# A graph layer on one core: the ReLU moves to VectorE, destinations' rows come from a table, 44 copied columns a step, updates part by part, a ring of twenty

## Chip, core and metric

One core of a Trainium2 chip. The metric is the device time of one execution in microseconds (us), lower is better; the kernel before was timed in three runs.

## What is computed

A graph layer over N = 12500 nodes of 64 features and E = 212500 edges, which come sorted by destination. The reference, cut to what matters:

```python
msg_in = concatenate([nodes[row], nodes[col], edge_features], axis=-1)   # 64 + 64 + 32
messages = relu(msg_in @ mW1 + mb1) @ mW2 + mb2                           # 128 hidden, 64 out
aggregated = segment_sum(messages, col, num_segments=12500)
upd = relu(concatenate([nodes, aggregated]) @ uW1 + ub1) @ uW2 + ub2
out = layernorm(x + upd)                                                  # no scale, eps 1e-5
```

Here `row` is the source of an edge (`src`), `col` its destination (`dst`). All data are fp32.

## The kernel before

**Groups.** Edges are worked in their order in G = 554 groups of 384 (three tiles of 128; the last group has two tiles, one of 20). Since edges are sorted, the destinations of a group lie in a window of W = 32 consecutive nodes. The kernel's host part passes the first destination of each group; a check on the chip (`ordered_edges`) finds out whether the windows hold, and another routine, `unordered`, runs if not. With these inputs `ordered` does the work.

**A step.** TensorE's work is written out by hand in steps. Step k does `turn(k)`, `hidden(k-2)` and `sums(k-4)`, each with its PSUM banks in two copies (`own.ps[g % 2]`). A step's first matmul carries all waits, and those who follow wait for its last one.

- `gather(g)` (L146 to 157): POOL fetches the source rows of a group with one indirect DMA per tile of 128 edges into `own.s`, a ring of RING = 8 groups; it is written AHEAD = 4 steps ahead. A new turn of the ring waits until the `turn` that read the old rows is done.
- `onehot(g)` (L329, VectorE): the place of each edge in its window as a one-hot row of 32, written beside the gathered rows.
- `turn(g)` (L341): TensorE transposes the 96 columns (64 features, 32 places) of each tile; ScalarE copies the result from PSUM into `own.st` (L351), where the edge features (`inputs`, L289) already lie below.
- `hidden(g)` (L366): one matmul per tile of `own.st` with `own.wm[g % 8]`. `wm` holds mW1's rows for the source (64), 32 rows with the projections of the window's nodes, and mW1's rows for the edge features (32). So the one-hot picks the destination's projection. ScalarE applies the ReLU into `own.h` (L377).
- `sums(g)` (L394, L399): matmuls of `h` with the one-hot add the group's hidden rows by destination, and count its edges. VectorE adds the window into `agg` (L406) and into a row of `own.xc` (L407), at a place taken from a register (`starts`, loaded by `places`).
- `places(b)` and `windows(b)`: for each block of four groups VectorE copies 4 x 32 nodes out of the transposed nodes `xc` (L308), TensorE projects them at the end of a step (L315), and VectorE copies 4 x 32 rows into `wm` (L320).

**Copied columns.** For some groups (`COPIED`) the first tile is not gathered. Its 128 columns are copied one by one from the transposed nodes `own.xc` to `own.st`, at addresses that are loaded into registers from a list of indices: `fetch(k)` (L475 to 507) has VectorE load 8 registers, copy 8 columns, load 12, copy 12, and ScalarE load 12, copy 12, load 8, copy 8 (VCOLS, ACOLS; loads L490, copies L503 and L505). COLS = 40 columns a step make a tile every 3.2 steps; 164 groups are served so. It begins with step 18 and ends before the last ten (SHORT), in which a step is cut into shorter ones.

**Updates.** When all edges of a chunk of 512 nodes are surely summed (`plan`), the update of the chunk is spread over steps (`step_update`): `load` brings the nodes, `first` does two matmuls (L424, L425), a ReLU on ScalarE (L427) and an add on VectorE (L428), `second` the outer matmuls (L437), an add (L439), the statistics (L443, L444) and a square root on ScalarE (L446), `third` scales (L451, L454) and stores (L458). Within one part an engine that follows waits for the one before it, in front of its own work for the step.

**Queues.** Each engine works its instructions in the written order. POOL has only the gathers after the start. SP issues the loads of edge features, of the nodes and source indices (`bit`, in the first 16 steps), of the lists, and the stores.

Of the kernel before, what the change touches and what calls it, by code (L numbers as in the profile page):

```python
# [34 lines left out]
AHEAD = 4  # L35
RING = AHEAD + 4
BLOCKS = 3
NW = 2 * SB
NH = 3
# [5 lines left out]
NEAR_GROUPS = 24  # L45
# [4 lines left out]
VCOLS = (8, 12)  # L50
ACOLS = (12, 8)
# [28 lines left out]
PLAN = plan()  # L80
COPIED = []
# [4 lines left out]
class Own:  # L86
# [4 lines left out]
    def __init__(self, nc, ctx):  # L91
# [10 lines left out]
        self.xc = on("own_xc", P, NP)  # L102

# [5 lines left out]
def ordered(ctx: ExitStack, tc: tile.TileContext, a, own, ok):  # L109
# [6 lines left out]
    xwp = ctx.enter_context(tc.tile_pool(name="xw", bufs=2))  # L116
# [6 lines left out]
    xc = own.xc[: D + 2]  # L123
    xc_bytes = own.xc.bitcast(U8)
# [20 lines left out]

    def gather(g):  # L146
        s = own.s[g % RING]
        loads[g] = [
            nc.gpsimd.indirect_dma_start(  # L149
                out=s[:p, j, :D], out_offset=None, in_=x[:, :],  # L150
                in_offset=bass.IndirectOffsetOnAxis(
                    ap=src_sb[:p, g * TG + j : g * TG + j + 1], axis=0),
            )
            for j, p in enumerate(tiles_of(g)) if j or g not in columned
        ]
        for i in loads[g]:
            after(i, *([turn_by[g // 2 * 2 + 1 - RING]] if g >= RING else []))
# [27 lines left out]
    nc.sync.dma_start(xc[D : D + 1, :].rearrange("o (p n) -> o p n", p=P), zero)  # L185
    nc.sync.dma_start(xc[D + 1 :, :].rearrange("o (p n) -> o p n", p=P), ones[:, : NP // P])
    w1b = const.tile([D + 2, H], F32, name="w1b")
    nc.vector.memset(w1b[D : D + 1, :], 0.0)
    nc.scalar.dma_start(w1b[:D, :], a["mW1"][D : 2 * D, :])
    nc.scalar.dma_start(w1b[D + 1 :, :], a["mb1"][None, :])  # L190
# [22 lines left out]
    nc.vector.memset(high[:, :NEAR_GROUPS], float(NEAR_NODES - W))  # L213
# [22 lines left out]
    ub1 = const.tile([H, 1], F32, name="ub1")  # L236
    nc.scalar.dma_start(ub1, a["ub1"][:, None])
    u2 = const.tile([H, D], F32, name="u2")
    nc.scalar.dma_start(u2, a["uW2"])
    u2b = const.tile([P, D], F32, name="u2b")  # L240
    nc.scalar.dma_start(u2b, a["ub2"][None, :].to_broadcast([P, D]))
    agg = const.tile([P, NP], F32, name="agg")
# [4 lines left out]
    starts, xws, indices, columns_by = {}, {}, {}, {}  # L247
# [3 lines left out]
    def combined():  # L251
# [5 lines left out]
        nc.vector.tensor_copy(ux[D : D + 1, :], wps[0:1, 1])  # L257
# [38 lines left out]
    def places(b):  # L296
# [8 lines left out]
        xw = xwp.tile([D + 2, SB, W], F32, name="xw")  # L305
        for i in range(n):
            starts[g + i] = v[i]
            nc.vector.tensor_copy(xw[:, i, :], xc[:, bass.ds(v[i], W)])  # L308
        xws[b] = xw, n

    def windows(b, wp, own_bank=True):


        xw, n = xws.pop(b)
        did = nc.tensor.matmul(wp[: n * W, :], xw[:, :n, :], w1b, start=True, stop=True)  # L315

        def copies():
            for i in range(n):
                g = b * SB + i
                c = nc.vector.tensor_copy(wm[g % NW][D : D + W, :], wp[i * W : (i + 1) * W, :])  # L320
                after(c, *([did] if own_bank else []), *([hidden_by[g - NW]] if g >= NW else []))
                wm_by[g] = c

        return did, copies
# [10 lines left out]
    def turn(g, ps):  # L335
# [9 lines left out]
        def copy(step):  # L345
# [5 lines left out]
                after(nc.scalar.activation(t[r, c : c + n][:, m], xt[r, m], AF.Copy), step)  # L351
# [9 lines left out]
    def hidden(g, ps):  # L361
# [11 lines left out]
        def relu(step):  # L373
            hidden_by[g] = step
            h = own.h[g % NH]
            if len(set(sizes)) == 1:
                relu_by[g] = [nc.scalar.activation(h, pre, AF.Relu)]  # L377
            else:
                relu_by[g] = [nc.scalar.activation(h[:p, j, :], pre[:p, j, :], AF.Relu)
                              for j, p in enumerate(sizes)]  # L380
# [6 lines left out]
    def sums(g, ps):  # L387
# [14 lines left out]
        def add(step):  # L402
            sums_by[g] = step
            at = bass.ds(starts.pop(g), W)
            return [
                after(nc.vector.tensor_tensor(agg[:, at], sg[:, 0, :], agg[:, at], ALU.add), step),  # L406
                after(nc.vector.tensor_tensor(xc[D : D + 1, at], counted,  # L407
                                              xc[D : D + 1, at], ALU.add), step),
            ]
# [3 lines left out]
    def update(base, p, n):  # L413
# [3 lines left out]
        def load():  # L417
            xin = up.tile([P, 4, D], F32, name="xin")
            nc.sync.dma_start(xin[:p, :n], x[rows, :].rearrange("(p n) d -> p n d", p=p))
            return xin  # L420

        def first(xin):
            u_ps = ups.tile([H, CH], F32, name="u_ps")
            nc.tensor.matmul(u_ps[:, :q], wc, agg[:, rows], start=True, stop=False)  # L424
            nc.tensor.matmul(u_ps[:, :q], ux, xc[: D + 1, rows], start=False, stop=True)  # L425
            u = up.tile([H, CH], F32, name="u")
            nc.scalar.activation(u[:, :q], u_ps[:, :q], AF.Relu, bias=ub1)  # L427
            nc.vector.tensor_tensor(xin[:p, :n], xin[:p, :n],  # L428
                                    u2b[:p].unsqueeze(1).to_broadcast([p, n, D]), ALU.add)
            return xin, u  # L430

        def second(xu):
            xin, u = xu
            o_ps = ups.tile([H, CH], F32, name="u_ps")[:, : 4 * D].rearrange(
                "p (n d) -> p n d", n=4)
            for k in range(n):
                nc.tensor.matmul(o_ps[:p, k], u[:, k:q:n], u2, start=True, stop=True)  # L437
            y = up.tile([P, 4, D], F32, name="y")
            nc.vector.tensor_tensor(y[:p, :n], o_ps[:p, :n], xin[:p, :n], ALU.add)  # L439
            stats = up.tile([P, 4, nc.vector.BN_STATS_DIM], F32, name="stats")  # L440
            mv = up.tile([P, 4, nc.vector.BN_AGGR_DIM], F32, name="mv")
            for k in range(n):
                nc.vector.bn_stats(stats[:p, k], y[:p, k])  # L443
                nc.vector.bn_aggr(mv[:p, k], stats[:p, k])  # L444
# [4 lines left out]
        def third(ymr):  # L449
# [10 lines left out]
        return [load, first, second, third]  # L460
# [14 lines left out]
    def fetch(k):  # L475
# [4 lines left out]
        if n == 0:  # L480
            indexes(i + 1)
        if n == SPAN - 2:
            addresses(i + 1)
        c0 = (k - BEGIN) * COLS
        for engine, count in [*((ET.DVE, c) for c in VCOLS), *((ET.Activation, c) for c in ACOLS)]:
# [9 lines left out]
            for q, at in zip(range(c0, c0 + count), v):  # L495
# [10 lines left out]
                after(by[engine], *([hidden_by[g - BLOCKS * SB]] if new else []))  # L506
            c0 += count
# [16 lines left out]
    def step(*work):  # L524
# [9 lines left out]
        copies = None  # L534
        for part, g, *_ in parts:
            if part is sums:
                for b in [b for b in xws if (b - 1) * SB <= g][:1]:
                    last, copies = windows(b, own.ps[g % 2][2][:, (TIMES + 1) * W :][:, :H])
                    did.append(last)
        for i in did[:-1]:  # L540
            tc.no_tile_sem_insts.add(i.ins.name)
            tc.add_to_no_dep_group("quiet", i.ins)
        for part, g, _, _, follow in parts:
            if part is sums:
                step_update(g)
            users[part][g % 2] = follow(did[-1])
            if part is sums and copies:
                copies()
                users[part][g % 2] += [wm_by[b * SB + i] for i in range(min(SB, G - b * SB))]
# [6 lines left out]
    windows(0, ups.tile([H, CH], F32, name="u_ps")[:, :H], False)[1]()  # L556
    indexes(0)
    made = summed = 0

    for k in range(G):  # L560
        if k < BITS:
            bit(k)
        if k == CHECKED:
# [361 lines left out]
```

## Time and profile before

| what | us |
|---|---|
| median of three runs | 1898.23 (1897.33 to 1900.16) |
| the profiled execution's own time | 1895.48 |
| its span (first to last instruction of the program) | 1893.5 |
| VectorE's wait for registers and the like ahead of L503 ("issue") | 217.9 |
| ScalarE's idle time ahead of the turn's copy (L351) | 205.8 |
| TensorE's idle time ahead of the transposes (L341) | 496.0 |
| granted TensorE clock, mean | 0.969 |

A group's row of the profile tells line, engine, operation, output from input, shape, the number of instructions, busy time and mean duration in ns, and then the engine's idle time just before them with what ended most of it ("issue": nothing that the profile shows). The timeline has start and length in us, with runs of like instructions merged; the brackets hold the idle time before. PE is TensorE's matmul row, PEld its weight loads, DVE VectorE, ACT ScalarE; a q behind the name is the engine's instruction queue.

### The profile page before, as it was taken

To read this page: it belongs to the slowest core of one execution; us is meant where nothing else is said; L and a number is where in the kernel's file an instruction comes from. 1 tells how busy PE (TensorE), PEld (TensorE's weight loads), DVE (VectorE), ACT (ScalarE), POOL (GpSimd) and SP (SyncE) were. 2 spreads that over 40 slices of the span, in tenths; PEclk is the share of its full clock that TensorE was granted. 3 is DMA by queue.
4 is the path that set the end of the run, shared out by engine and by line. 5 is a ranking of instruction groups with operands and counts; after the bars stand their busy time and mean duration, and the time that the engine had idled before them with its cause. 6 is when DMAs were issued, how large, how long until landed. Compare 5 with 4: busy or idle time off the path is not lost. (4 is left out here: it accounts for less than half of the span.)

```text
span 1893.5 us, 58044 instructions
## 1 busy us (share of the span) xinstructions
PE 1361.4 (72%) x12209; PEld 1193.4 (63%) x12209; DVE 1492.9 (79%) x13761; ACT 1550.7 (82%) x11818; POOL 1417.6 (75%) x1504
## 2 busy tenths in 40 slices
PE   3776777677777777677676776877767767767777
PEld 3666666666666666666665666666666656666665
DVE  3578888778888788887888878878888887888873
ACT  3489889888888888988988888889888888898882
POOL 7777777777777777777777777777777777777774
PEclk9999999999999999999999999999999999999999
DMA  6322222222222222222222222222222222222221
GB/s 136 73 46 45 46 48 44 50 43 48 46 45 48 47 43 50 45 46 44 48 50 43 48 46 45 46 48 44 50 44 47 47 48 44 47 44 50 44 47 29
DMA packets 68440, 92.50 MB, mean 49 GB/s; under 512 B 30893, under 2 KB 38350, under 8 KB 68078
## 3 DMA queue, kind: packets, MB, share of 16 engines
q0 software_dynamic: 47904, 49.12, 14.7%
q1 hardware_dynamic: 19260, 39.12, 7.4%
q14 instruction: 260, 2.13, 0.4%
q8 instruction: 102, 1.67, 0.4%
q10 hardware_dynamic: 914, 0.46, 0.1%
HBM read 85.29 MB, written 3.20 MB: 47 GB/s over the span
## 5 line engine op out<-in xcount | busy, mean ns | idle before, releaser
L149 POOL DMA_INDIRECT own_s<-in_x,src_sb x1497 | 1416.8, 946 | 457.3 <-issue 407.5
L503 DVE COPY own_st<-own_xc 64x4 uint8 x10500 | 897.7, 190 | 231.0 <-issue 217.9
L505 ACT ACTIVATE own_st<-own_xc 64x4 uint8 x10492 | 1057.1, 194 | 18.2 <-issue 15.2
L341 PE MATMUL own_ps<-own_ident,own_s 128*96 128x128 f32 x1661 | 289.5, 285 | 496.0 <-DMA own_s<-in_x,src_sb 157.9
L341 PEld LDWEIGHTS own_ps<-own_ident,own_s 128*96 128x96 f32 x1661 | 169.3, 132 | 566.1 <-ACT own_h L377 240.7
L394 PE MATMUL own_ps<-own_s,own_h 128*128 128x128 f32 x3322 | 480.5, 283 | 4.1 <-ACT own_h L377 2.9
L366 PE MATMUL own_ps<-own_wm,own_st 128*128 128x128 f32 x3322 | 479.4, 283 | 0.0
L351 ACT ACTIVATE own_st<-own_ps 96x384 f32<-96x384 f32 (+2 forms) x718 | 293.2, 408 | 205.8 <-PE own_ps L399 104.7
L394 PEld LDWEIGHTS own_ps<-own_s,own_h 128*128 128x128 f32 x3322 | 432.6, 199 | 6.3 <-ACT own_h L377 4.7
L366 PEld LDWEIGHTS own_ps<-own_wm,own_st 128*128 128x128 f32 x3322 | 432.1, 199 | 1.4 <-issue 0.5
L377 ACT ACTIVATE own_h<-own_ps 128x384 f32<-128x384 f32 x553 | 263.9, 477 | 16.0 <-PE own_ps L366 16.0
L399 PE MATMUL own_ps<-own_s,own_one 128*1 128x32 f32 x3322 | 190.1, 194 | 0.0
L320 DVE COPY own_wm<-own_ps 32x128 f32<-32x128 f32 x550 | 156.9, 285 | 5.6
L399 PEld LDWEIGHTS own_ps<-own_s,own_one 128*1 128x1 f32 x3322 | 114.5, 84 | 69.4 <-issue 6.2
L329 DVE TENSOR_TENSOR own_s<-iota,dlc 128x96 f32<-128x96 f32 x554 | 142.4, 258 | 14.3 <-issue 0.2
L406 DVE TENSOR_TENSOR agg<-own_ps,agg 128x32 f32 x554 | 105.1, 190 | 59.5 <-PE own_ps L399 25.9
L407 DVE TENSOR_TENSOR own_xc<-own_ps,own_xc 1x32 f32 x554 | 101.2, 183 | 30.6 <-PE u_ps L425 11.4
L308 DVE COPY xw<-own_xc 66x32 f32 x554 | 73.0, 207 | 15.5 <-DMA own_xc<-in_xT 9.8
L315 PE MATMUL own_ps<-w1b,xw 66*128 66x128 f32 (+1 forms) x276 | 69.1, 333 | 0.0
L446 ACT ACTIVATE rstd<-mv,eps 128x4 f32<-128x4 f32 (+1 forms) x25 | 7.4, 297 | 55.3 <-DVE mv L444 55.3
L437 PE MATMUL u_ps<-u,u 128*128 128x64 f32 (+1 forms) x196 | 50.1, 399 | 0.5 <-ACT u L427 0.5
L437 PEld LDWEIGHTS u_ps<-u,u 128*128 128x128 f32 (+1 forms) x196 | 47.1, 324 | 2.2 <-ACT u L427 0.9
(62 smaller groups left out, 276.7 us busy)
## 6 DMA issues: line engine op xcount, KB each, us to landing
own_st<-in_efT SPq DMA_DIRECT2D x138, 192.0 KB
own_s<-in_x,src_sb POOLq DMA_INDIRECT x1497
xin<-in_x SPq DMA_DIRECT2D x24, 128.0 KB
out<-o SPq DMA_DIRECT2D x24, 128.0 KB
own_xc<-in_xT SPq DMA_DIRECT2D x12, 179.2 KB
index<-in_src_copied SPq DMA_DIRECT2D x65, 1.2 KB
dlc_i<-in_dst_cols SPq DMA_DIRECT2D x1, 831.0 KB
own_xc<-in_xT SPq DMA_DIRECT2D x4, 179.5 KB
```

Source lines behind the costliest of these rows:

```text
L149: nc.gpsimd.indirect_dma_start(out=s[:p, j, :D], out_offset=None, in_=x[:, :], in_offset=bass.IndirectOffsetOnAxis(ap=src_sb[:p, g * TG + ...
L320: c = nc.vector.tensor_copy(wm[g % NW][D : D + W, :], wp[i * W : (i + 1) * W, :])
L329: places_by[g] = nc.vector.tensor_tensor(own.s[g % RING][:, :, D:], iota.unsqueeze(1).to_broadcast([P, TG, W]), dlc[:, g * TG : (g + 1) * ...
L341: nc.tensor.transpose(xt[:, j * P : j * P + p], s[:p, j, :], ident[:p, :p])
L351: after(nc.scalar.activation(t[r, c : c + n][:, m], xt[r, m], AF.Copy), step)
L366: nc.tensor.matmul(pre[:p, j, :], t[:, c + j * P : c + j * P + p], wm[g % NW], start=True, stop=True)
L377: relu_by[g] = [nc.scalar.activation(h, pre, AF.Relu)]
L394: did.append(nc.tensor.matmul(sg, h[:p, j, :], s[:p, j, D:].unsqueeze(1).to_broadcast([p, TIMES, W]), start=j == 0, stop=j == len(sizes) - 1))
L399: did.append(nc.tensor.matmul(counted, own.one[:p], s[:p, j, D:], start=j == 0, stop=j == len(sizes) - 1))
L406: after(nc.vector.tensor_tensor(agg[:, at], sg[:, 0, :], agg[:, at], ALU.add), step),
L503: by[engine] = nc.vector.tensor_copy(o, x_at)
L505: by[engine] = nc.scalar.activation(o, x_at, AF.Copy)
```

## The change

1. **ReLU.** VectorE applies it (`tensor_scalar` with max) instead of ScalarE.
2. **Columns.** VectorE 12 and 8, ScalarE 12 and 12: COLS = 44. VectorE's first twelve registers are loaded ahead of the add into `agg` (the list `between`), behind the ReLU; its first twelve copies come before the one-hot, the eight others after it. The list's load and address work go to the end of a step. `ordered_by_steps` takes the tool's own dependencies from the copies, which the steps order already.
3. **Destinations.** All nodes are projected once in 25 chunks of 512 (`projected`): one in each of the first 25 steps, two of them before, through the PSUM bank of the updates and ScalarE to a table in DRAM. For each group SP loads the 32 rows of its window into `wm` four steps ahead of its turn (`window`), at a row number from a register of SP. `LIMITS` keeps early windows within what is already in the table. The copies of nodes, the windows' matmul and the copies into `wm` go.
4. **Updates.** Six parts, one a step, each for one engine: `inner`, `relu`, `outer`, `stats`, `root`, `scaled`. The node and the bias enter the outer product by a matmul with an identity (`same`), so the load of the nodes and two adds go; the counts have a row of their own (COUNT) and a third inner matmul. The statistics are read from PSUM.
5. **Ring.** RING = 20, AHEAD = 16; a gather waits for the turn of its own slot.

`unordered` gets some of its space from `own.agg`; it isn't run here.

```diff
-AHEAD = 4
+AHEAD = 16
 RING = AHEAD + 4
-VCOLS = (8, 12)
-ACOLS = (12, 8)
+VCOLS = (12, 8)
+ACOLS = (12, 12)
...
-            after(i, *([turn_by[g // 2 * 2 + 1 - RING]] if g >= RING else []))
+            after(i, *([turn_by[g - RING]] if g >= RING else []))
...
+    def projected(c):
+        base, n = TABLE[c]
+        ps = ups.tile([H, CH], F32, name="u_ps").rearrange("p (n h) -> p n h", n=4)
+        for j in range(n):
+            nc.tensor.matmul(ps[:, j], xc[: D + 1, base + j : base + n * P : n], w1b,
+                             start=True, stop=True)
+        t = rowp.tile([P, 4, H], F32, name="t")
+        nc.scalar.activation(t[:, :n], ps[:, :n], AF.Copy)
+        written.append(after(nc.sync.dma_start(
+            by_dst[base : base + n * P, :].rearrange("(p n) h -> p n h", n=n), t[:, :n])))
+
+    def window(g):
...
+        wm_by[g] = nc.sync.dma_start(wm[g % NW][D : D + W, :],
+                                     by_dst[bass.ds(rows_at.pop(g), W), :])
+        after(wm_by[g], *written, *([hidden_by[g - NW]] if g >= NW else []))
+        written.clear()
...
-                relu_by[g] = [nc.scalar.activation(h, pre, AF.Relu)]
+                relu_by[g] = [nc.vector.tensor_scalar(h, pre, 0.0, None, ALU.max)]
...
+            count = xc[COUNT : COUNT + 1, at]
+            if between:
+                between.pop()()
+            a = after(nc.vector.tensor_tensor(agg[:, at], sg[:, 0, :], agg[:, at], ALU.add), step)
+            return [a, after(nc.vector.tensor_tensor(count, counted, count, ALU.add), step)]
...
         if k < G - SHORT:
+            between.append(lambda: registers(k, 0))
             step((turn, k), *([(hidden, k - 2)] if k > 1 else []),
                  *([(sums, k - 4)] if k > 3 else []))
             made, summed = max(0, k - 1), max(0, k - 3)
+            if between:
+                between.pop()()
+            fetch(0)
...
+        window(k + SB)
         onehot(k + 2)
-        fetch(k)
+        if k < G - SHORT:
+            for part in range(1, len(VCOLS + ACOLS)):
+                registers(k, part)
+                fetch(part)
```

More of the change, by code (lines that the diff above doesn't have):

```diff
@@ L144, in after, with ordered_by_steps @@
         return first
+    before = {}
+    def ordered_by_steps(i):
+        engine = i.ins.engine
+        tc.declare_no_dep(i.ins, group="features", keep=before.get(engine, []),
+                          reason="TensorE's step has read what the last turn of the ring wrote")
+        tc.add_to_no_dep_group("features", i.ins)
+        before[engine] = [i.ins]
+        return i
     def gather(g):
@@ L415, in update, with inner @@
         rows, q = slice(base, base + p * n), p * n
[L417 to L422, printed above, removed]
+        def inner():
             u_ps = ups.tile([H, CH], F32, name="u_ps")
             nc.tensor.matmul(u_ps[:, :q], wc, agg[:, rows], start=True, stop=False)
-            nc.tensor.matmul(u_ps[:, :q], ux, xc[: D + 1, rows], start=False, stop=True)
-            u = up.tile([H, CH], F32, name="u")
[L427 to L435, printed above, removed]
-            for k in range(n):
[L437 to L440, printed above, removed]
+            nc.tensor.matmul(u_ps[:, :q], ux, xc[: D + 1, rows], start=False, stop=False)
@@ L458, in third @@
             nc.sync.dma_start(out[rows, :].rearrange("(p n) d -> p n d", p=p), o[:p, :n])
-        return [load, first, second, third]
+        return [inner, relu, outer, stats, root, scaled]
     def indexes(i):
@@ L555, in ordered @@
     places(0)
-    windows(0, ups.tile([H, CH], F32, name="u_ps")[:, :H], False)[1]()
+    projected(0)
+    projected(1)
+    for g in range(SB):
+        window(g)
     indexes(0)
     made = summed = 0
+    between, held = [], {}
     for k in range(G):
```

154 lines of the change are left out of this document (83 added, 71 removed).

## The prediction

> **What bounds the kernel now.** I read the page's table of groups first, because its idle column tells who waits, then the instructions of the gather line alone, then the timeline of a few steps and of the end.
>
> ```profile
> PE 1361.4 (72%) x12209; PEld 1193.4 (63%) x12209; DVE 1492.9 (79%) x13761; ACT 1550.7 (82%) x11818; POOL 1417.6 (75%) x1504
> L149 POOL DMA_INDIRECT own_s<-in_x,src_sb x1497 | 1416.8, 946 | 457.3 <-issue 407.5
> L503 DVE COPY own_st<-own_xc 64x4 uint8 x10500 | 897.7, 190 | 231.0 <-issue 217.9
> ```
> By busy share ScalarE (82%) and VectorE (79%) look like the limits and POOL (75%) does not. But POOL's idle time is not waiting: 407.5 of its 457.3 us is "issue", 0.30 us between one gather and the next.
>
> ```profile
> L149 POOL DMA_INDIRECT own_s<-in_x,src_sb x1497: 901/944/1612, 2.9 to 1874.8; - x188
> ```
> Gathers run from 2.9 us to 1874.8 us. (1874.8 - 2.9) / 1496 = 1.2513 us from one start to the next, and in the timeline each gather of 0.94 us is followed by 0.30 us:
>
> ```profile
> 903.20 0.68 DVE L503 COPY own_st<-own_xc 64x4 uint8 x8
> 903.68 0.94 POOL L149 DMA_INDIRECT own_s<-in_x,src_sb  x1 [0.30 <-issue]
> 904.22 0.98 DVE L503 COPY own_st<-own_xc 64x4 uint8 x12 [0.34 <-issue]
> 904.25 2.00 ACT L505 ACTIVATE own_st<-own_xc 64x4 uint8 x20
> 904.93 0.95 POOL L149 DMA_INDIRECT own_s<-in_x,src_sb  x1 [0.30 <-issue]
> 905.12 0.19 DVE L406 TENSOR_TENSOR agg<-own_ps,agg 128x32 f32 x1
> 905.34 0.18 DVE L407 TENSOR_TENSOR own_xc<-own_ps,own_xc 1x32 f32 x1
> 905.56 0.26 DVE L329 TENSOR_TENSOR own_s<-iota,dlc 128x96 f32<-128x96 f32 x1
> 906.14 0.50 PE L341 MATMUL own_ps<-own_ident,own_s 128*96 128x128 f32 x3 [0.65 <-DMA own_s<-in_x,src_sb]
> 906.18 0.94 POOL L149 DMA_INDIRECT own_s<-in_x,src_sb  x1 [0.30 <-issue]
> ```
> So **POOL is saturated from end to end**, and TensorE's transposes wait for its data. Paired group by group, the transpose of a group starts 2.15 us (median; least 1.44) after its last gather instruction ended: nothing is far behind. 128 of each three or four groups' columns are not gathered but copied from the transposed nodes, 40 columns a step, which spares one gather in 128/40 = 3.2 steps: 3 - 0.3125 = 2.69 gathers a step, 3.363 us.
>
> The end: the last gather, the last transposes, the last store.
>
> ```profile
> 1874.83 0.90 POOL L149 DMA_INDIRECT own_s<-in_x,src_sb  x1 [0.30 <-issue]
> 1878.41 0.42 PE L341 MATMUL own_ps<-own_ident,own_s 128*96 128x128 f32 x2
> 1887.59 0.27 SPq L458 DMA_DIRECT2D out<-o  x1
> ```
> From the end of the last gather (1875.7) to the span's end (1893.5) are 17.8 us.
>
> **The change, part by part.**
>
> *24 columns on ScalarE, 20 on VectorE (44 for 40).* The list of copied tiles is a loop over constants: 164 entries at 40, 180 at 44. Gathers: 553 x 3 + 2 - 180 = 1481 for 1497. 16 x 1.2513 = **-20.0 us**, if POOL stays the bound. Its new step is (3 - 44/128) x 1.2513 = 3.324 us; every other engine must stay below it.
>
> *VectorE.* Removed per step: the copies into the window rows (L320, 156.9 us / 554 = 0.28), the copies of nodes (L308, 0.13), two adds per chunk of the update (L428, L439, 20 us in all, 0.04). Added: the ReLU on 128x384 from PSUM. Nearest rows: a PSUM copy of 128x128 takes 0.27 (L256), an add on 128x256 with one operand in PSUM 0.42 (L439); carrying their slope on gives 0.57; ScalarE does the same tile in 0.48 (L377). I take 0.55, with 0.41 and 0.60 as ends (0.41: half the slope of the copy). The engine's step: copies 0.98 + 0.68, less 0.16 hidden tails, 1.5; two adds 0.44 (0.22 from start to start); one-hot 0.26; ReLU 0.55; update work 2.7 us per 22.5 steps (four each of L443, L444, L454 and L451), 0.12; addresses 0.37 / 8 = 0.05. Together 2.92. On top come the register loads (L490 on the queue, median 0.84 for twelve). Before, the twelve came behind eight copies and showed as the 0.34 above. Now the eight are loaded behind twelve copies and the one-hot (1.2 us, longer than the 0.59 a load of eight takes), and the twelve behind the ReLU and the eight copies still queued: 0.84 + some 0.2 of register arithmetic against 0.55 + 0.3, so about 0.2 stays open. VectorE: 3.1 us, between 2.9 and 3.35. Steps of before without window copies took 2.76 and 2.86 us from transpose to transpose (903.38, 906.14, 909.00); with 0.55 more and up to 0.45 less of gap that gives the same.
>
> *ScalarE.* Loses the ReLU: 0.37 (start to start with the copy ahead of it). Gains four copies at 0.10 = 0.40. Its copies before ran as 20 in 2.00 with no gap, a load of twelve taking 0.77 behind eleven or more queued copies. New step: 24 x 0.10 + turn copy 0.43 = 2.8; if its queue has to wait for TensorE each step, two loads and the issuing of 24 copies bound it at about 3.0. Below 3.324.
>
> *TensorE* loses the windows' matmul and does the identity and the third inner product for the update; 2.07 us a step undisturbed (the starts of its transposes at 36.6, 38.75, 40.79), plus some 6 us of update per chunk (L424 1.05, L425 0.9, L437 2.0, and as much again for the identity) / 22.5 = 0.3: 2.4. Free.
>
> *Updates a step apart.* Before, ScalarE stood 55.3 us before the square roots and VectorE 22.1 before the sums, all under POOL: **0 us** here. If POOL were not the cover, they would be worth up to their 77 us.
>
> *Rows of destinations from a table.* 25 chunks are projected (8 matmuls, by L315's 0.49 for two: 2.0 us), copied by ScalarE (0.69, as L427), stored, and read back by SP, 554 transfers of 32 rows, issued six steps before use (20 us), against some 3 us from issue to landing for a small transfer (the last store: 1887.59 to its last packet at 1890.3). On SP each stands behind the transfers of edges, stores and indices; these wait for steps that are already past. In the steady state 0. In the first 25 steps TensorE runs 2.07 + 2.0, more where SP holds the next piece of nodes behind the wait for a stored chunk; I put it at 4.6 us a step.
>
> *Ring of twenty, 16 ahead.* POOL never waited, so this gains nothing by itself. It pays for the start: POOL may begin group g + 20 when group g is turned. At 3.754 (three gathers) up to group 20 and 3.324 after, it wants group 24 turned at 158 us. TensorE: step 2 at about 36 us (the table's first chunks wait for the 10.7 us zeroing of the sums on ScalarE that ends at 23.9), 22 x 4.6, and 6 us for the checks at step 8: 143 us. Bounds 4.1 and 7 us a step: no loss, or up to 38 us less what the 6-step lead of the windows gives back; I take 0.
>
> *The tail* keeps its chain; 0.3 us of an add leaves, matmuls of the same size come: 0, +-1.5.
>
> **A rule weighed against the trace.** L308 is an fp32 copy within SBUF, and 554 of them go. In the trace, after 100 us, the 192 gathers with such a copy beside them are 1252 ns from start to start, the others 1250 (median 1249 both).
> The Trainium skill (SBUF — State Buffer, "Who interferes with whom") says that such a copy takes the ports through which POOL writes a gather's descriptors and that whoever comes second is blocked for the whole instruction. By that rule removing them would give POOL up to their 73.0 us back, and the sum would be -93; the trace disagrees, with 2 ns for 1252.
>
> **Sum.** 1893.5 - 20.0 = 1873.5 us of span. The profiled execution's own time was 1895.5, the median of the runs 1898.2: I add the same 4.7 us and forecast **1878 us**. Its own range: 1873 (a pitch of 1.249, no outliers: -3.5; tail -1.5) to 1884 (a few us at the start).
>
> **Rivals.**
> 1. *The start stalls POOL.* If the first steps take 5.3 us or more ((158 - 42) / 22) instead of 4.6, POOL finds its ring full near group 44 and never gets this back. At 6.0: 36 + 132 + 6 - 158 = 16 us, 1894. For it: SP issues the pieces of nodes, the table's stores and the windows in order, and VectorE waited until 30.2 us for a piece issued at 25.3 or 26.4. Against: 15 us of margin. Typically 5 to 12 us: 1883 to 1890.
> 2. *VectorE becomes the bound (slower).* Place: its queue, which must wait for TensorE's step ahead of the ReLU before it can load registers (in the trace no load starts behind a waiting add; the least is 0.22 after it). Some 524 steps with copies: span = 1873.5 + 524 x (step - 3.324). From 3.36 it is slower than before. If the eight queued copies are no cover, 0.84 + 0.2 - 0.55 = 0.5 stays open: 2.92 + 0.5 = 3.42, a span of 1924, a time of 1929; with nothing covered 3.9 and 2180 at worst. For it: 79% busy plus 218 us of gaps now. Against: the sum of 3.1, and the twelve have the ReLU as cover.
> 3. *POOL freed of the L308 copies.* If each held a gather up for its whole time, 73.0 us come back beside the 20.0: 1893.5 - 93.0 + 4.7 = 1805, for half of it 1842. Against it stand the 2 ns. It is what the page's rule gives.
> 4. *It doesn't do what it says*: a table row late on SP each step would stop TensorE; with a lead of 20 us a transfer would need to take seven times the 3 us. Within rival 2's times, a part of its chance.
>
> **Chances.** Forecast 0.62; rival 1 0.14 (two thirds of it still a gain, a third within 0.2%); rival 2 with 4 0.18 (0.15 slower, 0.03 no difference, where the step lies near 3.36); rival 3 0.03 and other gains 0.03. A difference under 0.2% (3.8 us) can't be told from none here. Faster 0.62 + 0.09 + 0.06 = 0.77; same 0.05 + 0.03 = 0.08; slower 0.15. The range 1868 to 1906 holds the forecast, rival 1 and the near part of rival 2.
>
> **What would show it.** Right: 1481 gathers, still 1.25 us apart with 0.30 of "issue" and no other releaser; the ReLU near 0.55 on VectorE; VectorE's gaps smaller than 218 us; last gather near 1855. Wrong: gathers waiting for TensorE's transposes (early, before 200 us: rival 1; throughout: rival 2); a pitch of 1.1 (rival 3); transposes waiting for the table's rows (rival 4).

## The result, and the profile after

The changed kernel takes 1877.05 us (median of four runs, 1876.62 to 1877.49); the kernel before, in the same session, 1897.78. The ratio is 0.9893, with an interval of 0.988 to 0.9905. The profiled execution has a span of 1874.9 us for 1893.5. The last eight experiments met chips on which the kernel before itself took 2545 to 2668 us, with a granted clock of 0.78 to 0.82 where it was 0.97 here; their times are compared only with that and say little of these 20 us.

The page's row of engines and its groups, kernel after (columns as before):

```profile
PE 1429.1 (76%) x12373; PEld 1252.6 (67%) x12373; DVE 1491.0 (80%) x13140; ACT 1552.1 (83%) x13372; POOL 1399.1 (75%) x1488
L165 POOL DMA_INDIRECT own_s<-in_x,src_sb x1481 | 1398.4, 944 | 452.5 <-issue 303.3
L541 ACT ACTIVATE own_st<-own_xc 64x4 uint8 x12560 | 1268.1, 192 | 64.3 <-issue 56.0
L539 DVE COPY own_st<-own_xc 64x4 uint8 x10480 | 893.8, 190 | 20.8 <-issue 1.1
L406 DVE TENSOR_SCALAR own_h<-own_ps 128x384 f32<-128x384 f32 x553 | 302.0, 546 | 141.4 <-PE own_ps L428 97.3
```

Sixteen gathers fewer, the ReLU as a new group of VectorE with 546 ns each, and VectorE's idle time ahead of its copies down from 231.0 to 20.8 us. VectorE's and ScalarE's busy shares hardly moved (79 to 80%, 82 to 83%), and POOL's idle time went from 457.3 to 452.5. VectorE's idle time didn't go with the gaps ahead of the copies: a part of it moved ahead of the add into `agg` (L406 of the kernel before, L437 of the kernel after), where the load of twelve registers now stands:

```profile
L406 DVE TENSOR_TENSOR agg<-own_ps,agg 128x32 f32 x554 | 105.1, 190 | 59.5 <-PE own_ps L399 25.9 <-PE own_ps L315 20.3 <-PE u_ps L424 12.4
L437 DVE TENSOR_TENSOR own_agg<-own_ps,own_agg 128x32 f32 x554 | 106.0, 191 | 147.2 <-DVE own_h L406 95.1 <-issue 22.8 <-PE own_ps L428 10.3
```

In 306 of the 554 steps the add waits over 0.1 us and starts within 0.3 us of the end of a load; these waits come to 122 us.

The waits of POOL, kernel after (total us, number, longest):

```profile
POOL own_s L165 <- issue: 303.3, 995, 0.3
POOL own_s L165 <- DMA own_s<-in_x,src_sb: 116.1, 381, 0.3
POOL own_s L165 <- PE own_ps L428: 27.7, 91, 0.3
```

More of the gaps now carry the name of a transfer or of TensorE than before (36.6 and 10.1 us), where the prediction expected no other releaser than "issue". That is only what the profile happens to find in the same 0.3 us: the longest gap is 0.3 us in each row, and the timeline of the steps shown before has the gathers as close as ever:

```profile
902.46 0.94 POOL L165 DMA_INDIRECT own_s<-in_x,src_sb  x1 [0.31 <-issue]
...
903.03 1.02 DVE L539 COPY own_st<-own_xc 64x4 uint8 x12
903.71 0.94 POOL L165 DMA_INDIRECT own_s<-in_x,src_sb  x1 [0.30 <-issue]
...
904.23 0.66 DVE L539 COPY own_st<-own_xc 64x4 uint8 x8
904.40 2.38 ACT L541 ACTIVATE own_st<-own_xc 64x4 uint8 x24
904.81 0.54 DVE L406 TENSOR_SCALAR own_h<-own_ps 128x384 f32<-128x384 f32 x1
904.96 0.94 POOL L165 DMA_INDIRECT own_s<-in_x,src_sb  x1 [0.30 <-issue]
905.57 0.19 DVE L437 TENSOR_TENSOR own_agg<-own_ps,own_agg 128x32 f32 x1 [0.22 <-DVE own_h L406]
```

VectorE's copies, one-hot and ReLU follow each other without a gap for a register load (the add that comes next, at 905.57, stands 0.22 us behind the ReLU's end); ScalarE's 24 copies are one run of 2.38 us. POOL still sets the pace. The gather line alone, and the end:

```profile
L165 POOL DMA_INDIRECT own_s<-in_x,src_sb x1481: 898/944/1353, 2.9 to 1851.5; - x186
```

```profile
1851.51 0.90 POOL L165 DMA_INDIRECT own_s<-in_x,src_sb  x1 [0.30 <-DMA own_s<-in_x,src_sb]
...
1857.26 0.42 PE L369 MATMUL own_ps<-own_ident,own_s 128*96 128x128 f32 x2
...
1867.28 0.30 SPq L490 DMA_DIRECT2D out<-o  x1
```

**Where the 18.6 us of span come from.**

| term | us |
|---|---|
| 16 gathers fewer at 1.2513 | -20.0 |
| start to start 1.2490 instead of 1.2513 us, 1481 times | -3.4 |
| end of the last gather to the end of the span: 22.5 instead of 17.8 | +4.7 |

The second term is for the most part a few long gathers that are gone: after the first 40 us the kernel before has 14 over 985 ns (3.0 us over 944 ns in all), the kernel after 2 (0.2 us). Of the third, 2.2 us lie between the end of the last gather and the last transposes (2.7 before, 4.85 after), 0.8 in the chain from there to the last store's issue, and 1.7 behind that issue (7.6 instead of 5.9). The last part goes with the program: it is 5.9 to 6.0 us in the two runs of the kernel before with 44 columns too, and 7.5 to 7.7 in the runs of the kernel after with 40 columns, with the ReLU on ScalarE, with the short ring, with fewer gathers and with 48 columns at good addresses. What causes it stays open.

**The start.** The transposes of groups 0, 24 and 60 start at 26.1, 134.9 and 249.6 us, so the steps with the table took (134.9 - 26.1) / 24 = 4.53 us on the mean; most of them took 4.0, and the mean holds the 10.3 us from group 1 to group 2, and the 10.4 and 5.95 around the checks (groups 7 to 9). In groups 10 to 60 TensorE is 33 to 41 us behind the gathers, some ten groups; POOL, with its lead of sixteen, doesn't notice. Then the engines run at their own pace, seen in the transposes (rows of TensorE, kernel after):

```profile
249.62 0.50 PE L369 MATMUL own_ps<-own_ident,own_s 128*96 128x128 f32 x3 [0.56 <-issue]
252.62 0.51 PE L369 MATMUL own_ps<-own_ident,own_s 128*96 128x128 f32 x3 [0.89 <-issue]
255.56 0.50 PE L369 MATMUL own_ps<-own_ident,own_s 128*96 128x128 f32 x3 [0.83 <-ACT own_st L541]
```

Steps of 3.00 and 2.94 us here, 3.11 on the mean of groups 60 to 150, against POOL's 3.319. No single engine is full there: from 250 to 530 us ScalarE is busy for 91%, VectorE for 87% and TensorE for 80% of the time. Near group 200 the lag is made up and stays at 1.5 to 6 us.

### The profile page after: what moved, and what is told of

Same layout as the page of the kernel before. It is cut to its first block, busy times and chain, and to the rows that moved or that the text cites. A ratio compares the mean times of both kernels' runs of the same rounds, so it can differ in the third digit from the quotient of the medians.

```text
span 1874.9 us, 61070 instructions
## 1 busy us (share of the span) xinstructions
PE 1429.1 (76%) x12373; PEld 1252.6 (67%) x12373; DVE 1491.0 (80%) x13140; ACT 1552.1 (83%) x13372; POOL 1399.1 (75%) x1488
## 5 line engine op out<-in xcount | busy, mean ns | idle before, releaser
L165 POOL DMA_INDIRECT own_s<-in_x,src_sb x1481 | 1398.4, 944 | 452.5 <-issue 303.3
L541 ACT ACTIVATE own_st<-own_xc 64x4 uint8 x12560 | 1268.1, 192 | 64.3 <-issue 56.0
L539 DVE COPY own_st<-own_xc 64x4 uint8 x10480 | 893.8, 190 | 20.8 <-issue 1.1
L406 DVE TENSOR_SCALAR own_h<-own_ps 128x384 f32<-128x384 f32 x553 | 302.0, 546 | 141.4 <-PE own_ps L428 97.3
L437 DVE TENSOR_TENSOR own_agg<-own_ps,own_agg 128x32 f32 x554 | 106.0, 191 | 147.2 <-DVE own_h L406 95.1
L428 PE MATMUL own_ps<-own_s,own_one 128*1 128x32 f32 x3322 | 188.8, 194 | 0.0
L428 PEld LDWEIGHTS own_ps<-own_s,own_one 128*1 128x1 f32 x3322 | 113.6, 83 | 69.1 <-issue 4.9
L331 PE MATMUL u_ps<-w1b,own_xc 65*128 65x128 f32 x196 | 52.0, 416 | 30.9 <-DMA own_wm<-in_mW 16.3
L331 PEld LDWEIGHTS u_ps<-w1b,own_xc 65*128 65x128 f32 x196 | 47.2, 324 | 33.2 <-DMA own_wm<-in_mW 16.2
L462 PE MATMUL u_ps<-u,u 128*128 128x64 f32 (+1 forms) x196 | 63.1, 405 | 0.5 <-ACT u L456 0.5
L463 PE MATMUL u_ps<-same,own_xc 65*128 65x64 f32 (+1 forms) x196 | 62.3, 403 | 0.0
L462 PEld LDWEIGHTS u_ps<-u,u 128*128 128x128 f32 (+1 forms) x196 | 54.2, 325 | 2.4 <-ACT u L456 0.8
L463 PEld LDWEIGHTS u_ps<-same,own_xc 65*128 65x128 f32 (+1 forms) x196 | 54.9, 328 | 0.0
```

What stands on the lines that cost most here:

```text
L165: nc.gpsimd.indirect_dma_start(out=s[:p, j, :D], out_offset=None, in_=x[:, :], in_offset=bass.IndirectOffsetOnAxis(ap=src_sb[:p, g * TG + ...
L406: relu_by[g] = [nc.vector.tensor_scalar(h, pre, 0.0, None, ALU.max)]
L428: did.append(nc.tensor.matmul(counted, own.one[:p], s[:p, j, D:], start=j == 0, stop=j == len(sizes) - 1))
L462: nc.tensor.matmul(y[:p, k], u[:, k:q:n], u2, start=True, stop=False)
L463: nc.tensor.matmul(y[:p, k], xc[: D + 1, base + k : base + q : n], same, start=False, stop=True)
L539: by[engine] = nc.vector.tensor_copy(o, x_at)
```

## The experiments

All are the kernel after with the edit shown, except where the kernel before is named.

**Is it the columns alone?**

```diff
-ACOLS = (12, 12)
+ACOLS = (12, 8)
```

> The changed kernel with ScalarE copying 20 columns of 40 again (12 and 8). Theory (POOL alone sets the time): 1497 gathers instead of 1481 at 1.249 us each, +20 us on the changed kernel's 1877: 1897, as before the change; POOL still 1.25 us from gather to gather with only the 0.30 us of issue between. Rival (the other parts bring the gain, the ReLU or the updates a step apart): near 1877, or at least clearly under 1890.

Measured: 1897.97 us, ratio 1.0005 (0.9995 to 1.0014); 1497 gathers at a mean of 1.2495 us, the last ending at 1873.1, and a tail of 22.7 us. With 40 columns the other four parts of the change are worth nothing in time, although they take VectorE's gaps ahead of its copies away here too (20.9 us left, with 153.4 ahead of the add). Beside this the two small terms can be seen by themselves: the gathers end 2.6 us earlier than in the kernel before, and the tail is 4.9 us longer. So both belong to the other parts, not to the columns.

**Does the ReLU have to move?**

```diff
-                relu_by[g] = [nc.vector.tensor_scalar(h, pre, 0.0, None, ALU.max)]
+                relu_by[g] = [nc.scalar.activation(h, pre, AF.Relu)]
...
```

> The changed kernel with the ReLU on ScalarE, all else kept. Theory (POOL bounds only while every other engine's step stays under its 3.319 us; ScalarE's step is 3.0 to 3.1 with 24 columns, and the ReLU brings 0.37): ScalarE's step comes to about 3.45, ScalarE bounds, the gathers wait for transposes once the ring is full, 1877 + 524 x 0.13 = 1945 (range 1890 to 1965). Rival (ScalarE has room, the move of the ReLU hides under POOL like everything else): 1877.

Measured: 1879.69 us, ratio 0.9907 (0.989 to 0.9923): the theory fell, the rival stood. ScalarE's rows (engine row and its copies):

```profile
PE 1424.3 (76%) x12373; PEld 1242.7 (66%) x12373; DVE 1239.1 (66%) x12585; ACT 1714.6 (91%) x13927; POOL 1401.4 (75%) x1488
L541 ACT ACTIVATE own_st<-own_xc 64x4 uint8 x12560 | 1253.5, 201 | 2.7 <-issue 2.3
```

ScalarE is 91% busy and has 2.7 us of idle time ahead of its copies, yet its step is 3.19 us (mean of groups 60 to 150), not the 3.45 that I had added up. The loads of registers run on its queue while earlier copies are still being worked, and the ReLU is one more cover for them: the trace has a load of 0.78 us starting in the middle of the copies in each step. The price is the lag, which is made up only near group 350 instead of 200. The time is 2.6 us above the kernel after's, 2.2 of it in a start to start of 1.2505 us for 1.2490; why isn't shown.

**What does the ring pay for?**

```diff
-AHEAD = 16
+AHEAD = 4
```

> The changed kernel with AHEAD = 4, a ring of eight. Theory (the long ring pays only for the slow first 25 steps): in the changed kernel's trace the transposes of group 23 start 17.6 us after POOL would need their slot in a ring of eight, so POOL stalls there: 1877 + 17.6 = 1895, all of it lost before 150 us, and no stall later. Rival (the ring gains nothing, as POOL never waited before): 1877. Rival (the ring is needed all along, against jitter): clearly over 1900, with stalls after 200 us.

Measured: 1899.41 us, ratio 1.0015 (1.0005 to 1.0024): the gain is gone. The wait of POOL on TensorE, and the first long stall in the timeline:

```profile
POOL own_s L165 <- PE own_ps L428: 52.5, 118, 7.1
```

```profile
62.42 0.94 POOL L165 DMA_INDIRECT own_s<-in_x,src_sb  x1 [0.30 <-issue]
70.49 0.94 POOL L165 DMA_INDIRECT own_s<-in_x,src_sb  x1 [7.12 <-PE own_ps L428]
```

All long stalls lie between 62 and 165 us; the last gather ends at 1872.0, 19.6 us later than with the long ring. What POOL loses at the start it never gets back, since it has no slack to catch up with. The table slows the first 25 steps, and the ring of twenty pays for exactly that.

**What comes next behind POOL?** From group 20 on the third tile of a group isn't gathered; its rows keep what an earlier turn of the ring left there.

```diff
-            for j, p in enumerate(tiles_of(g)) if j or g not in columned
+            for j, p in enumerate(tiles_of(g)) if (j or g not in columned) and (j != 2 or g < RING)
```

> The changed kernel without the gather of each group's third tile from group 20 on (its rows keep what an earlier turn of the ring left); POOL then needs about 2.1 us a step. Theory (the next bound is ScalarE's and VectorE's step of 3.12 us, as in the changed kernel's steps 30 to 140, in which TensorE is still behind POOL): turn of group 24 at 135 us, 519 x 3.12 more, then the tail: 1800 (1780 to 1815), with POOL waiting for transposes. Rival (the distance between groups 30 and 140 still comes from the start, the engines could go at 2.8 to 2.9 as single steps do): 1640 to 1690.

Measured, one run: 1804.10 us, 73 us below the kernel after. Now POOL waits for TensorE through the whole run:

```profile
POOL own_s L165 <- PE own_ps L428: 656.9, 454, 6.0
```

The steps are 3.10 us on the mean from group 60 on (3.06 to 3.13 in stretches of 90 to 100), as in the stretch in which the kernel after catches up. So POOL's number of gathers is the bound of the kernel after, and the other engines' next limit is 3.1 us a step.

**44 columns in the kernel before.**

```diff
-ACOLS = (12, 8)
+ACOLS = (12, 12)
```

> The kernel before with nothing changed but ScalarE's columns, 12 and 12 instead of 12 and 8: 44 a step, ReLU still on ScalarE, windows projected as before, ring of eight. Theory A (only the number of gathers counts): 1481 gathers at 1.2513, 1897.6 - 20 = 1878, like the whole change. Theory B (the other parts are what makes 44 possible: ScalarE's step of 2.74 goes to 3.14, to which its waits for VectorE and TensorE in the updates, 82 us in all, add 0.15 and more, and a ring of eight can't lend): steps often over 3.32, POOL waits for transposes, 1884 to 1900.

> The kernel before with ACOLS (12, 12) and nothing else: 44 columns, 1481 gathers instead of 1497. Theory (POOL alone sets the pace, and its time is the number of gathers times a start-to-start of 1.250 us): 1898 - 16 x 1.25 = 1878 us (1875 to 1882), POOL with no wait over 0.4 us on an instruction of TensorE after the start; then all other parts of the change weren't needed for the gain. Rival (the old engines' step, with ReLU and 24 copies on ScalarE and the window copies on VectorE, doesn't keep up with a POOL step of 3.32 us): over 1884 us, up to 1910, with the gathers waiting several us at a time on L399 (the ring of eight covers four steps).

Measured, on two chips: 2607.14 us beside 2544.79 (ratio 1.0239, 1.0184 to 1.0295) and 2610.07 beside 2548.54 (1.0256, 1.0217 to 1.0294). There POOL isn't the bound (second run; 619.9 us in the first):

```profile
POOL own_s L149 <- PE own_ps L399: 633.2, 188, 8.0
```

Where the engines set the pace, four more columns on a ScalarE that also has the ReLU cost time, as they should. Whether they would on a chip where POOL sets it, the question of this pair, is not answered.

**VectorE's adds and POOL's gathers.** A hundred adds of 128x256, four in each chunk's update, once with both operands in SBUF, once with one of them in PSUM (`iota` in place of `extra[1]`):

```diff
...
             nc.scalar.activation(u[:, :q], u_ps[:, :q], AF.Relu)
+            for _ in range(4):
+                nc.vector.tensor_tensor(extra[2], extra[0], extra[1], ALU.add)
```

> The changed kernel with four adds on VectorE of two 128x256 operands in SBUF in the update part that has only ScalarE's ReLU (100 adds in all, results unused), of the kind of L428 in the kernel before. Theory (such an add, and not the load of nodes beside it, made the long gathers of before: 7 of its 25 stood within 0.13 us of the start of a gather of 1.1 to 1.4 us): the four last about 1.7 us and meet a start in each chunk, so some 20 to 30 gathers of over 1.0 us, together 4 to 9 us, and 1881 to 1886. Rival (the long gathers have another cause): no gather over 1.05 after the start, 1877.

> The same with one operand of the four adds in PSUM; same number, shape and place. Theory (two operands in SBUF are what holds a gather up): no long gathers, 1877 to 1878. If the adds cost by VectorE's time instead, both kernels come out alike and above 1877.

Times: 2413.08 (0.9464, 0.9417 to 0.951) and 2417.41 us (0.9477, 0.943 to 0.9524) beside the same 2544.79; no difference between them. The gathers themselves can be read: over 985 ns were 12 (2.09 us over 944 ns in all) with both operands in SBUF, 3 (0.26 us) with one in PSUM. Nine of the twelve (1.67 us) begin within 0.25 us of an add; the other three, the three of the second run and both of the kernel after begin 0.05 to 0.14 us behind the address arithmetic on the list (`addresses`), an instruction that all of these kernels have. So the count that bears on the theory is 9 against 0: of the adds that begin within 0.25 us of a gather's beginning, 9 of 26 lengthened it with both operands in SBUF, and none of 30 with one in PSUM. The direction is the theory's; 20 to 30 gathers and 4 to 9 us were expected. One of the nine:

```profile
801.32 1.26 POOL L165 DMA_INDIRECT own_s<-in_x,src_sb  x1 [0.30 <-issue]
801.34 1.79 DVE L461 TENSOR_TENSOR extra<-extra,extra 128x256 f32<-128x256 f32 x4
```

The gather that starts 0.02 us ahead of the adds takes 1.26 us for 0.94. Both kernels are 5% faster than the kernel before on that chip, where 44 columns alone were 2% slower: where the engines are the bound, the other parts of the change do pay.

**More columns.** First two on VectorE and two on ScalarE:

```diff
-VCOLS = (12, 8)
-ACOLS = (12, 12)
+VCOLS = (12, 10)
+ACOLS = (14, 12)
```

> The changed kernel with 48 columns: VectorE 12 and 10, ScalarE 14 and 12. POOL's step becomes (3 - 48/128) x 1.249 = 3.279. Theory (POOL bounds as long as the others stay below; their step was 3.12 and grows by some 0.15 for two columns each): 1465 gathers or so, 16 x 1.249 = 20 less, 1857. Rival (step of the others reaches POOL's): 1865 to 1890, with POOL waiting for transposes.

Measured: 2805.90 us, ratio 1.1002 (1.0946 to 1.1059), while the kernels with the extra adds, on the same chip, had 0.95. ScalarE's loads of 14 registers took 3.03 us each, those of 12 0.78. Fourteen seemed to be too many, so the next had 46 columns, none of its lists longer than 12:

```diff
-VCOLS = (12, 8)
+VCOLS = (12, 10)
```

> The kernel after with VCOLS (12, 10): 46 columns a step, copies and registers grow by two on VectorE. A tile every 128/46 steps: some 1473 gathers, POOL's step (3 - 46/128) x 1.249 = 3.298 us instead of 3.318. Theory (the pace is POOL's, the other engines' step is 3.12 us and grows by 2 x 0.09 us of copies and some 0.1 us of loading registers to 3.2 to 3.4, so it is close): 1867 us if they keep up, and 1867 to 1890 if VectorE's step is at 3.3 or over; the first is taken, 1868. Rival (VectorE's step rises over POOL's): over 1880, and waits of the gathers on L428 of more than 0.4 us through the whole run.

Measured: 2918.16 us, ratio 1.1474 (1.143 to 1.1519), worse still. The rows of ScalarE in the timeline, and the loads of both engines (least, median and greatest ns):

```profile
1502.92 1.25 ACT L541 ACTIVATE own_st<-own_xc 64x4 uint8 x12 [1.78 <-issue]
1505.92 1.25 ACT L541 ACTIVATE own_st<-own_xc 64x4 uint8 x12 [1.75 <-issue]
1507.19 0.66 ACT L380 ACTIVATE own_st<-own_ps 32x128 f32<-32x128 f32 x2
1507.75 2.38 ACT L541 ACTIVATE own_st<-own_xc 64x4 uint8 x24
```

```profile
L520 DVEq TENSOR_LOAD <-index x1047: 844/1147/3130, 171.4 to 2853.8; - x175
L520 ACTq TENSOR_LOAD <-index x1046: 771/2577/3237, 171.4 to 2850.2; - x175
```

ScalarE's columns weren't touched, and yet one step has its 24 copies in one run, as in the kernel after, and another has gaps of 1.75 us. Sorted by step, ScalarE's loads of twelve take 2.605 us (median) in every even step and 0.784 in every odd one. What alternates is the address: a step's list is 46 x 4 = 184 bytes long, ScalarE's parts begin at 88 and 136 bytes, so that they lie 8 bytes off a multiple of 16 in each even step. In all kernels with 40 or 44 columns every part begins at a multiple of 16. The last run tests this with a longer list at such addresses:

```diff
-ACOLS = (12, 12)
+ACOLS = (12, 16)
```

> The kernel after with ACOLS (12, 16): 48 columns, every list of registers a multiple of four at an address that is a multiple of 16 bytes. Some 1465 gathers, 16 fewer than the kernel after. Register loads: theory (a load is fast where its numbers come in whole, aligned groups of four; 12 took 0.784 us at such an address and 2.605 us at one 8 bytes off): all of ScalarE's loads of 12 take 0.78 us, those of 16 about 0.543 + 2 x 0.24 = 1.02 us, none over 1.1; rival (a longer list is slow by itself): those of 16 take 2 to 3.5 us. Time: the other engines' step is 3.12 us with VectorE's ReLU and was 3.19 with the ReLU on ScalarE (0.48 us more there); four more copies on ScalarE are 0.4 us, so 3.15 to 3.25. Theory (POOL still sets the pace, at a step of (3 - 48/128) x 1.249 = 3.279 us): 1877 - 16 x 1.249 = 1857 us. Rival (the engines' step comes to 3.25 or more, the lag of the start is never made up): 1865 to 1890, with the transposes some 30 us behind the gathers to the end. Expected 1860. All this against a kernel before of 1898 us; where that takes about 2545, only the register loads are read.

Measured: ScalarE's loads of 16 registers took 1.020 us (median), those of 12 0.783; together (least, median, greatest ns):

```profile
L520 ACTq TENSOR_LOAD <-index x1045: 774/1007/1427, 170.2 to 2411.5; - x175
```

The theory of the address stands, and the longer list isn't slow by itself. The time, 2480.73 us beside 2668.26 (ratio 0.9291, 0.9246 to 0.9336), can't say whether 48 columns beat 44 where POOL is the bound; nor was the kernel with 44 run beside it on this chip.

**Is the longer tail TensorE's load?** The identity's matmuls and the counts' own inner matmul are left out; the output lacks the node, the second bias and the counts' term.

```diff
-            nc.tensor.matmul(u_ps[:, :q], ux, xc[: D + 1, rows], start=False, stop=False)
-            nc.tensor.matmul(u_ps[:, :q], uc[COUNT : COUNT + 1, :], xc[COUNT : COUNT + 1, rows],
-                             start=False, stop=True)
+            nc.tensor.matmul(u_ps[:, :q], ux, xc[: D + 1, rows], start=False, stop=True)
...
-                nc.tensor.matmul(y[:p, k], u[:, k:q:n], u2, start=True, stop=False)
-                nc.tensor.matmul(y[:p, k], xc[: D + 1, base + k : base + q : n], same,
-                                 start=False, stop=True)
+                nc.tensor.matmul(y[:p, k], u[:, k:q:n], u2, start=True, stop=True)
```

> The kernel after without the identity matmuls of the updates (L463) and without the counts' own inner matmul (L450): the output lacks x, ub2 and the counts' term. It takes 25 x (4 x 0.4 x 2 + 1.05) = some 100 us of work off TensorE. Theory (TensorE has that room everywhere but in the last steps, where its work sits behind the last gather): the stretch from the end of the last gather to the end of the span falls from 22.5 us to 19 to 20.5, the pace of the gathers stays at 1.249 us, and the time is 1873 to 1875. Rival (the tail is a chain of waits and not TensorE's load): 1877, the stretch 22 us or more. A second rival (TensorE's load slows the steps): the gathers' pace changes, and the time falls below 1870.

Measured: 2394.03 us, ratio 0.9395 (0.9372 to 0.9419), with a tail of 73 us, because POOL is there some 57 us ahead of TensorE at the end. That tail isn't the one in question, so the experiment leaves the cause open.

## Why the prediction was right, point by point

**POOL is the bound, and the columns are its price.** Right, and shown from three sides: with 40 columns the gain is gone, with a third of the gathers left out 73 us more come off, and in the result the gathers are 1481 with gaps of 0.3 us. The term of -20.0 us is borne out by a run: from the kernel after with 40 columns to that with 44 the last gather ends 20.7 us earlier (1873.1 and 1852.4), and the spans differ by 20.9.

**Start to start.** Taken as unchanged at 1.2513 us; it fell to 1.2490, which is worth 3.4 us. This was the low end of the range, not the value taken. The long gathers that went were for the better part the updates' adds: seven of the fourteen, with 2.1 of the 3.0 us, begin within 0.13 us of the beginning of an add at L428, which the change removes, as here (kernel before):

```profile
351.84 1.23 POOL L149 DMA_INDIRECT own_s<-in_x,src_sb  x1 [0.30 <-issue]
351.84 0.41 DVE L428 TENSOR_TENSOR xin<-xin,u2b 128x256 f32<-128x256 f32 x1
```

The two experiments with added adds support the cause. The rival that gave POOL the 73 us of the copies at L308 back was rightly given 3%: only three of the fourteen long gathers have such a copy starting within a microsecond of them, and one of these three has an add beside it as well. For the adds the Trainium skill (SBUF — State Buffer, "Who interferes with whom") says that a VectorE instruction with two inputs in SBUF contends with a GpSimd instruction that reads SBUF, and that one with at most one such input, outside the two-port modes, does not. The 9 against 0 agree; but here it shows only where the two begin nearly together, and costs 0.16 to 0.42 us in the kernel before.

**VectorE.** Predicted 3.1 us a step; 3.11 measured while the engines run freely, but that is the step of all engines: VectorE's own work is 2.72 us of it (87%), where 2.92 was added up. The ReLU, not in the trace of before, was put at 0.55 and took 0.546. Of the loads, those of eight are hidden as expected (20.8 us of gaps ahead of the copies are left of 231.0); those of twelve were to leave "about 0.2" open, and the idle time ahead of the add is 0.21 us a step from 250 to 500 us.

**ScalarE.** 2.8 to 3.0 was expected. Its busy time is 2.84 us a step from 250 to 530 us; a step of its own isn't seen, since 3.11 is the step of all engines. With the ReLU put back the step is 3.19, so the change's first part was not needed for 44 columns. The prediction hadn't claimed that it was, but my own expectation for that run did, at 1945 us: it added the loads and the ReLU up, where one covers the other.

**Table and ring.** 4.6 us a step and 6 us for the checks were estimated from step 2 on, 107 us to group 24; it took 97.8 (37.1 to 134.9), most steps 4.0. (The three starts that the prediction gives for TensorE's undisturbed step come to 2.10 us, not 2.07; nothing hangs on it.) Group 24 was expected turned at 143 us and was at 134.9. So the first rival (POOL stalled at the start) had 158 - 134.9 = 23 us of margin against it rather than 15. That the ring gains nothing itself and pays for the start is shown by the run with a ring of eight. The steady state of the table, 0, is covered by the run with 40 columns.

**Updates a step apart: 0.** Also covered by that run, in the sum with the rest.

**The tail.** The step that failed: 0 +-1.5 was predicted, +4.7 measured. "Matmuls of the same size come" was nearly right for the chain from the last transposes to the last store's issue (+0.8), but the term left out what TensorE has to do beside it in the last ten, short steps. The prediction had priced the identity's matmuls at another 2.0 us a chunk and spread them over 22.5 steps as free; in the last steps they aren't. There TensorE works the outer product of the chunk before, with the identity's matmuls between (rows of TensorE's transposes, outer and identity matmuls, kernel after; the pairs between and TensorE's other work are cut):

```profile
1841.49 0.49 PE L369 MATMUL own_ps<-own_ident,own_s 128*96 128x128 f32 x3
1843.43 0.68 PE L462 MATMUL u_ps<-u,u 128*128 128x64 f32 x2
1843.95 0.63 PE L463 MATMUL u_ps<-same,own_xc 65*128 65x64 f32 x2
...
1846.76 0.63 PE L463 MATMUL u_ps<-same,own_xc 65*128 65x64 f32 x2
1848.18 0.85 PE L369 MATMUL own_ps<-own_ident,own_s 128*96 128x128 f32 x3
```

From transposes to transposes this step takes 6.69 us. Its eight outer and eight identity matmuls fill 1843.43 to 1847.39, 3.96 us, half of them new. In the kernel before the same chunk's outer product fills 2.08 us, in a step of 4.94:

```profile
1866.33 2.08 PE L437 MATMUL u_ps<-u,u 128*128 128x64 f32 x8
```

TensorE doesn't get the 1.9 us back before the last transposes, which come 4.85 us after the last gather instead of 2.7. This reading is from the traces; the run that was to prove it couldn't. It would account for 2.2 of the 4.7 us. The 1.7 behind the last store's issue, which the prediction took to stay, lie behind all of TensorE's work, and their cause is open.

The two misses, -3.4 and +4.7, nearly cancel: 1873.5 - 3.4 + 4.7 gives a span of 1874.8, and 1874.9 was measured. The median of the runs after lies 2.2 us above its profiled span, where I had added 4.7. So the mechanism and the main term were right, but that the forecast of 1878 is only 1 us off is in part luck: -3.4, +4.7 and -2.5 happen to sum to -1.2.

## What to carry to other kernels

Where one engine works without a gap, count its instructions: what makes them fewer is the gain, and everything else, even an engine's 200 us of gaps, can at most make room for that (here the move of the ReLU wasn't needed; whether 44 columns alone would have done isn't shown); check that the others still fit below its pace. An engine with no slack never makes up a stall, so a slow start must be bridged by a buffer as long as the lag (here ten groups). And when numbers are loaded from a list into registers, keep every piece a multiple of four at a multiple of 16 bytes.

## What the runs showed of the hardware

**Loads of registers.** Start addresses counted within the list; medians in us:

| registers | at a multiple of 16 bytes | 8 bytes off |
|---|---|---|
| VectorE, 8 | 0.596 | |
| VectorE, 12 | 0.848 | 2.736 |
| VectorE, 10 | 1.075 | 2.297 |
| ScalarE, 12 | 0.783 | 2.605 |
| ScalarE, 14 | | 3.027 |
| ScalarE, 16 | 1.020 | |

Four aligned numbers cost about 0.24 us (1.020 - 0.783), little more than a single one 8 bytes off (0.21 to 0.22, from the differences of the right column): ten aligned cost two groups and two singles. The Trainium skill (Runtime: NRT & Kernel Launch, "Instruction fetch mechanics") gives some 200 ns for each register, for loads from HBM. These lists lie in SBUF; the loads that are 8 bytes off come near it (217 ns each for ScalarE's twelve), the aligned ones take a third of that (65 ns).

**A pair of short windows.** In the kernel before, two-operand adds in SBUF on VectorE lengthened a gather of POOL only where both begin within 0.13 us: all seven that do, none of the other eighteen. In the run with added adds it took a beginning within 0.25 us, and most of those that close (17 of 26) left no mark. Two operands aren't the whole condition: gathers of 0.04 to 0.17 us more than 0.944 also stand beside instructions with one tensor operand in SBUF, the address arithmetic on a list and, in the kernel before, the scaling at L454.
